# A graph attention layer on one core: four products of zero weights a block between spreading q[dst] and k; the last nodes split into early units and tiles of 128 rows; powers ahead of the copies of rows

## The chip, the cores and the metric

The kernel runs on one core of a Trainium2 chip. The metric is the device time of one execution in microseconds (us); a time is given as the median of several executions. The core has five engines, each with an instruction stream of its own: TensorE (PE; its weight loads are listed as PEld), VectorE (DVE), ScalarE (ACT), GpSimd (POOL) and SyncE (SP), which here issues most of the DMAs. A core has 16 DMA engines.

## The reference

12,500 nodes of 128 features, 212,500 edges sorted by their destination `dst`, 8 heads of 16 features. With h = relu(layernorm(x)):

```python
q, k, v = h @ Wq.T + bq, edge_attr @ Wk.T + bk, h @ Wv.T + bv
in_m   = sum(q[src] * k)        # per edge and head
out_m  = sum(q[dst] * k)
diag_m = sum(q[src] * q[dst])
score = (segsoftmax(in_m / 4) + segsoftmax(out_m / 4) + segsoftmax(diag_m / 4)) * weight ** lam
y = segment_sum(score[..., None] * v[dst], dst) @ Wo.T + bo
out = x + leaky_relu(y, 0.1)
```

`segsoftmax` is a softmax over the edges of one destination. Inputs and outputs are float32.

## The kernel before

**Stages.** `ordered_path` first computes layernorm and q of all nodes and writes q to a table in DRAM (until about 160 us). Then comes the loop over the edges, which takes most of the time, and then the end of the program behind the loop, called the tail here. Beside it stands a general path, which runs only if the data have not the expected order.

**The loop.** The edges lie in 5 segments (S) of 83 tiles (G), and one block is 512 edges of one segment: `for g in range(end)` with 415 blocks, segment s = g % 5, tile t = g // 5. The iteration of block g computes the logits of block g and prepares what later blocks need:

- POOL: `gather(g + 23)`, four indirect DMAs (L696) that fetch q[src] of 128 edges each into a tile `qq`. Each is made to start behind a certain product of PE: `behind[g, 0]` to `behind[g, 3]` are the ends of `spread_q`, `project`, `turn` and of the rest of the iteration.
- PE: `spread_q(g + 1)` (L1201), four bf16 products of one-hot rows `oh` with a window of the q table, which put q[dst] and the bias of k into the two halves of `kq_ps` (a PSUM tile of two banks, two such tiles in turn); then `project(g + 1)` (L1190), float32 products that add edge_attr @ Wk into the k half; then `turn(g + 2)` (L1183), four transposes of edge rows into `eT_ps` (one such tile).
- ACT: the copy `eT` (L1185) of `eT_ps`, which `project` of the next iteration reads; the copy `qd` (L1194) of q[dst], behind `project`; the one-hot rows `relb`, `oh` (L1177, L1178).
- DVE, `logits(g)`: the products `prod` of qd with k (L1215) and of qq with both halves of `kq_ps` (L1216); every second block the sums over 16 features, `lT` (L1220).

Spread over the five blocks of a tile lies the work on whole tiles, for tiles that are one to three behind: `turn_logits` transposes `lT` into `l_ps` (L1241), two scans (L1274, L1292) find the running maximum of each destination from both sides, `turn_max` turns it back (`m_ps`, L1366), `powers` takes the exponentials (`back`, L1376 and L1377), `weigh_powers` multiplies them by the weights (L1387), `show_ends` makes the selection `sel` (products `d_ps`, L1402), `to_rows` sums the exponentials of each destination by 16 products (`w_ps`, L1417) and copies them out (`rows`, L1423), and `put_rows` writes windows of 38 node rows for each segment to the DRAM tables `sums` (L1434).

**The nodes.** Units of 256 nodes are worked off by `Nodes` objects, two units (four tiles of 128 rows) each: `load_sums` reads numerators and denominators (L1088; L1090 where a unit lies on the border of two segments and has two parts), `scores_of` divides (L1057 to L1063), `product` computes v by a bias product and four float32 products (L1113, L1115), `hold` does this into a PSUM place that is kept, `weigh` multiplies v by the scores (L1123), `turn` transposes (L1107), `project_o` multiplies by Wo (the same two product lines), `take_larger` and `add_x` finish (L1138, L1142), `store` writes (L1148, L1150). Of 25 such objects 20 are worked off within the loop, from t = 18 on. The others, `rest`, are [18,9], [10,19], [28,29], [38,39] and [48]: their x is loaded and normalized within the last 12 blocks (`begin_rest`), their sums are loaded behind the last rows.

**What sets the order.** Every instruction is pinned: each engine runs its instructions in the order in which the code writes them, and waits on semaphores where data or a buffer are needed. SP issues its DMAs in the same order. The order of the tail is thus the order of the calls at the end of `ordered_path`, and the places of the loop's products that of the calls within the loop.

Of the kernel before, what the change touches and what calls it, by code (L numbers as in the profile page):

```python
# [16 lines left out]
HEADS = 8  # L17
# [455 lines left out]
def ordered_path(ctx: ExitStack, tc: tile.TileContext, flag, x, src, dst, edge_attr, edge_weight,  # L473
# [48 lines left out]

    def parts_of(u):

        return [s for s in range(S)
                if (s == 0 or START * s - NEAR < UN * (u + 1))
                and (s == S - 1 or UN * u <= START * (s + 1) + NEAR)]

    def stored_at(u):

        of = parts_of(u)
        t = -(-(UN * (u + 1) + NEAR - START * of[0]) // RATE)
        return t + 2 if len(of) == 1 and t < T else None

# [7 lines left out]
    sums = [dram.tile([NP, 2, 2 * H3], F32, name=f"sums{i}") for i in range(S)]  # L542

# [43 lines left out]
    worst = consts.tile([RW, 1], F32, name="worst")  # L587
    LEAD, RAW, AHEAD = 3, 15, 11
# [467 lines left out]
    def scores_of(ab, score):  # L1056
        pin(nc.vector.tensor_add(ab[:, :, 0, :], ab[:, :, 0, :], ab[:, :, 1, :]))  # L1057
        den, num = ab[:, :, 0, 0:H3], ab[:, :, 0, H3:]
        pin(nc.vector.tensor_scalar(den, den, 1e-30, None, op0=ALU.max))
        pin(nc.vector.reciprocal(den, den))  # L1060
        pin(nc.vector.tensor_mul(num, num, den))
        pin(nc.vector.tensor_add(score, num[:, :, 0:HEADS], num[:, :, HEADS:2 * HEADS]))
        pin(nc.vector.tensor_add(score, score, num[:, :, 2 * HEADS:]))  # L1063

    class Nodes:
# [13 lines left out]
        def load_sums(self, to=None, more=None):  # L1079
            self.ab = fin.tile([P, JN, 2, 2 * H3], F32, name="ab", bufs=3) if to is None else to  # L1080
            for i, u in enumerate(self.of):
                both = slice(2 * i, 2 * i + 2)
                of = parts_of(u)

                def rows(s):
                    return (sums[s][u * UN:(u + 1) * UN].rearrange("(p k) i c -> p k (i c)", p=P))

                pin(nc.sync.dma_start(self.ab[:, both].rearrange("p k i c -> p k (i c)"), rows(of[0])))  # L1088
                if len(of) > 1:
                    pin(nc.sync.dma_start(more[:, both].rearrange("p k i c -> p k (i c)"), rows(of[1])))  # L1090
# [49 lines left out]
        def add_x(self, engine):  # L1140
            v, y = self.held[:, :self.n], self.x[:, :self.n]
            pin(engine.tensor_add(y, v, y))  # L1142

        def store(self):
            for i, u in enumerate(self.of):
# [3 lines left out]
                else:  # L1149
                    pin(nc.sync.dma_start(out[u * UN:, :].rearrange("(p k) f -> p (k f)", k=2),  # L1150
                                          y[:LAST, :]))


# [4 lines left out]
    rest = [u for _, u in todo] + [u for u in range(NU) if stored_at(u) is None]  # L1158
    rest = [Nodes(rest[i:i + 2]) for i in range(0, len(rest), 2)]

    with tc.tile_pool(name="work", bufs=2) as work, \
# [43 lines left out]

        def logits(g):
# [7 lines left out]
            prod = prods[0][:, :, s - lo]  # L1214
            pin(nc.vector.tensor_mul(prod[:, :, 2, :], qds[g], kqs[g][:, :, 1, :]))  # L1215
# [3 lines left out]
            if s % 2 == 0 or alone:  # L1219
# [7 lines left out]
        ends_ab = scan.tile([P, len(rest) * JN, 2, 2 * H3], F32, name="ends_ab", bufs=1)  # L1227
# [95 lines left out]
        def examine():  # L1323
# [31 lines left out]
            pin(nc.vector.tensor_reduce(found[:, 3:4], found[:, 0:3], AX.X, ALU.max))  # L1355
            pin(nc.vector.tensor_copy(flag, found[:, 3:4]))
# [13 lines left out]
        def powers(t):  # L1370
            d = st[t]
            back = d["back"] = work.tile([P, JN, S, 2, H3], F32, name="back")
# [79 lines left out]
        def nodes_between(t, s):  # L1452
# [17 lines left out]
            if old and even and s == 2:  # L1470
                old.take_larger()
                old.add_x(nc.vector)
# [6 lines left out]
        assert len(rest) <= len(starts)  # L1479
# [5 lines left out]
        def begin_rest(at):  # L1485
            if at in turned:
                late.update(zip(turned[at], halves(len(turned[at]))))
            for r, (of, begin) in enumerate(zip(rest, starts)):
                if at == begin:
                    to, of.h = halves()  # L1490
                    of.load_x(to)
# [5 lines left out]

            if at == BEGIN - 1:
                for of in rest:
                    of.more = None  # L1500
                    if any(len(parts_of(u)) > 1 for u in of.of):
                        more = gath.tile([P, JN, F], F32, name="qq").rearrange("p j f -> p (j f)")
                        of.more = more[:, :of.n * 4 * H3].rearrange(
                            "p (k i c) -> p k i c", k=of.n, i=2)
                        pin(nc.gpsimd.memset(of.more, 0.0))
# [28 lines left out]
        for g in range(end):  # L1534
# [5 lines left out]
            if g + 1 < end:  # L1540
                spread_q(g + 1)
                behind[g + 1, 0] = pinned[products]
                project(g + 1)
# [28 lines left out]
            elif t < G - 1:  # L1572
                later(to_rows, t - 2)
# [21 lines left out]
            if g == end - 1:  # L1595
                last_pair.turn(small([P, JN, P], "node_ps"))
                more_banks()
            if g < S:
                of = [u for u in range(NU) if g in parts_of(u)]
# [126 lines left out]
```

## Time and profile before

| what | value |
|---|---|
| median of 3 runs | 2637.92 us (2632.82 to 2642.26) |
| the profiled execution's own time | 2642.74 us |
| its span, first to last instruction | 2640.9 us |
| mean granted TensorE clock | 0.786 of full speed |
| last gather of q[src] issued | about 2472 us |
| last put of rows issued | 2603.65 us |
| last addition on DVE ends | 2633.85 us |
| last store issued | 2634.72 us |

Before about 162 us the tables are made; to about 2588 us the loop runs; behind it lies the tail. The profile's page lists each engine's busy time, the granted clock (`PEclk`) in 40 slices of the span, and groups of instructions by line; lists of waits name, for each engine and line, what ended the idle time ahead of it.

### The profile page before, as it was taken

What the parts mean: (1) busy time and instruction counts of PE and PEld (TensorE: products, weight loads), DVE (VectorE), ACT (ScalarE), POOL (GpSimd) and SP (SyncE); (2) the same over time, 40 slices, a digit from 0 to 9 for tenths busy, and PEclk for the clock granted to TensorE, in tenths of its full rate; (3) what the DMA queues carried; (4) which work ended last, traced back from release to release, by engine and by line L of the source; (5) the groups of instructions that cost most, each with busy time, mean ns of one, the idle gap of its engine ahead of it and who ended that gap; (6) DMA issues with size and microseconds to landing.
All of it is one profiled execution on the core that took longest, in us unless ns stands there. A gap on an engine that the chain in (4) does not pass through costs nothing.

```text
span 2640.9 us, 34648 instructions
## 1 busy us (share of the span) xinstructions
PE 1657.0 (63%) x9986; PEld 1406.9 (53%) x9986; DVE 2002.2 (76%) x2205; ACT 1422.5 (54%) x2742; POOL 1587.3 (60%) x1678
## 2 busy tenths in 40 slices
PE   5655656565665566666666666565666666666677
PEld 4544545454555455555555565454555555555665
DVE  6656777777787777777878777777877787778896
ACT  6644555455555555555555555555554555555572
POOL 6666666666666666666666666666666666666200
PEclk9876777778777887877878777878877787778786
DMA  8464444444444444444444444444444444444431
GB/s 235 143 202 130 132 121 121 145 131 121 129 147 132 131 132 148 140 132 130 134 139 144 126 134 144 144 122 130 146 139 129 124 145 139 120 126 133 122 91 53
DMA packets 306303, 355.74 MB, mean 135 GB/s; under 512 B 118433, under 2 KB 225899, under 8 KB 305795
## 3 DMA queue, kind: packets, MB, share of 16 engines
q1 hardware_dynamic: 238340, 238.99, 29.8%
q0 software_dynamic: 53184, 108.92, 15.0%
q10 hardware_dynamic: 14580, 5.53, 0.8%
q8 instruction: 82, 1.34, 0.2%
q14 instruction: 117, 0.96, 0.1%
HBM read 321.41 MB, written 31.85 MB: 134 GB/s over the span
## 4 chain that ended last, share of the span: by engine, by line
PE 31%; ACT 22%; another core or an unknown queue 17%; issue 14%; DVE 10%; DMA 0%; DVEq 0%; POOL 0%; ACTq 0%; SPq 0%; POOLq 0%
PE kq_ps L1190 11%; PE w_ps L1417 6%; PE kq_ps L1201 5%; ACT qd L1194 4%; ACT eT L1185 4%; PE eT_ps L1183 4%; ACT relb L1177 4%; DVE lT L1220 3%; DVE prod L1216 3%; ACT oh L1178 2%; PE node_ps L1115 2%; ACT sel L1406 2%; ACT sel L1405 2%; ACT back L1377 1%
## 5 line engine op out<-in xcount | busy, mean ns | idle before, releaser
L696 POOL DMA_INDIRECT qq<-q_table,src_i x1600 | 1517.2, 948 | 852.1 <-issue 368.8
L1190 PE MATMUL kq_ps<-wk,eT 128*128 128x128 f32 x3320 | 627.3, 348 | 677.0 <-ACT eT L1185 478.3
L1190 PEld LDWEIGHTS kq_ps<-wk,eT 128*128 128x128 f32 x3320 | 554.3, 252 | 757.7 <-ACT eT L1185 526.3
L1220 DVE TENSOR_REDUCE lT<-prod 128x192 f32<-128x3072 f32 (+1 forms) x250 | 702.3, 2809 | 8.5
L1194 ACT COPY qd<-kq_ps 128x512 f32<-128x512 f32 x415 | 242.0, 583 | 723.2 <-remote 443.9
L1216 DVE TENSOR_TENSOR prod<-qq,kq_ps 128x1024 f32<-128x1024 f32 x415 | 504.0, 1214 | 0.0
L1215 DVE TENSOR_TENSOR prod<-qd,kq_ps 128x512 f32<-128x512 f32 x415 | 283.1, 682 | 179.5 <-issue 97.5
L1201 PE MATMUL kq_ps<-win,oh 114*128 114x256 bf16 x1660 | 296.5, 307 | 96.8 <-issue 44.5
L1185 ACT COPY eT<-eT_ps 128x512 f32<-128x512 f32 x415 | 244.5, 589 | 174.8 <-remote 117.0
L1183 PE MATMUL eT_ps<-ident,ea 128*128 128x128 f32 x1660 | 321.4, 329 | 5.6 <-issue 5.6
L1177 ACT ACTIVATE relb<-relb,before 114x512 bf16<-114x512 bf16 x415 | 301.8, 727 | 0.0
L1201 PEld LDWEIGHTS <-oh 114*128 114x128 bf16 x1660 | 178.1, 111 | 172.6 <-issue 136.8
L1178 ACT ACTIVATE oh<-relb 114x512 bf16<-114x512 bf16 x415 | 261.5, 630 | 13.2
L1183 PEld LDWEIGHTS eT_ps<-ident,ea 128*128 128x128 f32 x1660 | 258.8, 175 | 6.2 <-issue 6.2
L1417 PE MATMUL w_ps<-back,sel 128*114 128x144 f32 (+1 forms) x1312 | 208.6, 323 | 72.4 <-ACT sel L1406 52.7
L1387 DVE TENSOR_TENSOR back<-back,m_ps 128x480 f32<-128x480 f32 x84 | 54.9, 653 | 256.1 <-ACT back L1377 239.3
L1417 PEld LDWEIGHTS w_ps<-back,sel 128*114 128x114 f32 x1312 | 194.3, 219 | 99.4 <-ACT sel L1406 72.7
L1274 DVE TENSOR_TENSOR_SCAN u<-far,u,l_ps 120x512 f32<-120x512 bf16 x82 | 104.5, 1275 | 30.0 <-PE kq_ps L1201 12.4
L1292 DVE TENSOR_TENSOR_SCAN m<-far_ps,head,u 120x512 f32<-120x512 f32 x81 | 103.9, 1282 | 8.4
L1423 ACT COPY rows<-w_ps 114x240 f32<-114x240 f32 x84 | 29.8, 355 | 129.1 <-PE kq_ps L1201 43.3
L696 POOL DMA_INDIRECT qq<-in_x_dram,raw_i x60 | 61.5, 1024 | 35.7 <-issue 15.6
L1366 PE MATMUL m_ps<-ident,m 120*128 120x120 f32 x332 | 70.1, 351 | 5.5 <-DVE m L1292 2.8
(196 smaller groups left out, 1458.8 us busy)
## 6 DMA issues: line engine op xcount, KB each, us to landing
ea<-in_edge_attr_dram SPq DMA_DIRECT2D x83, 1280.0 KB
relb<-rel_d SPq DMA_DIRECT2D x83, 640.0 KB
qq<-q_table,src_i POOLq DMA_INDIRECT x1600
win<-q_table SPq DMA_DIRECT2D x415, 28.5 KB
far<-far_d SPq DMA_DIRECT2D x84, 120.2 KB
q_table<-more_q SPq DMA_DIRECT2D x40, 192.0 KB
sums<-rows SPq DMA_DIRECT2D x408, 7.1 KB
q_table<-xq SPq DMA_DIRECT2D x24, 256.0 KB
```

Of the source, the lines that this page charges most:

```text
L696: rows = pin(nc.gpsimd.indirect_dma_start(out=qq[:, j, :], out_offset=None, in_=x if g < RAW else q_table, in_offset=bass.IndirectOffsetOn ...
L1177: pin(nc.scalar.activation(d, d, AF.Abs, bias=before[:K3]))
L1178: pin(nc.scalar.activation(oh, d, AF.Relu, bias=1.0, scale=-1.0))
L1183: pin(nc.tensor.transpose(eT_ps[:, j, :], eas[g // S][:, g % S, j * F:(j + 1) * F], ident))
L1185: pin(nc.scalar.copy(eT, eT_ps))
L1190: pin(nc.tensor.matmul(kqs[g][:, j, 1, :], eTs[g][:, j, :], wk, start=False, stop=(j % 2 == 1)))
L1194: pin(nc.scalar.copy(qds[g], kqs[g][:, :, 0, :]))
L1201: pin(nc.tensor.matmul(kq[:, j].rearrange("p i f -> p (i f)"), ohs[g][:, j * P:(j + 1) * P], win[:, s:S + 1:S - s, :], start=(j % 2 == 0), ...
L1215: pin(nc.vector.tensor_mul(prod[:, :, 2, :], qds[g], kqs[g][:, :, 1, :]))
L1216: pin(nc.vector.tensor_mul(prod[:, :, 0:2, :], qqs[g][:, :, None, :].to_broadcast([P, JN, 2, F]), kqs[g]))
L1220: pin(nc.vector.tensor_reduce(lTs[t][:, :, lo:s + 1, :].rearrange("p j s c -> p j (s c)"), prods[0][:, :, :s + 1 - lo].rearrange("p j s i ...
L1417: pin(nc.tensor.matmul(w_ps[:, own[0]:own[-1] + 1, :].rearrange("p s c -> p (s c)"), d["sel"][:n, j, lo:lo + TRIO, :].rearrange("p s w -> ...
```

## The change

Line numbers of the kernel after the change are given with "after".

**Zero products.** A new function `add_nothing(g + 1, 2)` is called in each iteration between `spread_q` and `project` (after: L1278). It issues four bf16 products of 512 columns, two into each bank of the block's `kq_ps`; their weights are the low halves of the float32 identity matrix, which are zero, so they add zero. The first gather of an iteration is still tied to the end of `spread_q`, the second to that of `project`.

**The last nodes.** The borders between segments are now cut at fixed nodes (`CUTS`: 2474, 4974, 7472, 9972), chosen so that a unit's sums lie in one table from a cut on, but for a few nodes around the cut. These are worked off by a new class `Ends`: four tiles of 128 rows, one at each cut, at addresses that are read from the data (`end_bases`, filled in `examine`), whose sums of both tables are added. Their statistics of layernorm go through DRAM (`stats_d`). 21 objects of two units are now worked off in the loop, one more than before (an additional one at t = 14). `rest` is three objects of units 18, 9, 19, 28, 29 and 38, beside `whole` (unit 48) and `ends`.

**The tail.** The sums of the three objects and the second tables' sums of `ends` (14 loads) are now issued ahead of the last three tiles' puts, behind the last put only 5 loads follow (4 of `ends`, 1 of `whole`). `to_rows(G - 3)` moves into the last block's iteration, the products of two held objects ahead of the last `to_rows`, `powers` of the last two tiles ahead of `to_rows(G - 2)`. The last block's sums over features are made in two pieces, the first ahead of the second logits product.

```diff
@@ the loop
                 spread_q(g + 1)
                 behind[g + 1, 0] = pinned[products]
+                add_nothing(g + 1, 2)
                 project(g + 1)
                 behind[g + 1, 1] = pinned[products]
...
-            elif t < G - 1:
+            else:
                 later(to_rows, t - 2)
@@ new
+        halves_of_one = ident.bitcast(BF)
+        nothing = halves_of_one[:, 0:2 * P:2]
+        something = halves_of_one[:, None, :].to_broadcast([P, JN // 2, 2 * P])
+
+        def add_nothing(g, times):
+
+            for i in range(times):
+                for j in range(0, JN, 2):
+                    pin(nc.tensor.matmul(kqs[g][:, j:j + 2].rearrange("p j i f -> p j (i f)"),
+                                         nothing, something, start=False, stop=False))
@@ class Ends
+        def rows(self, t, s):
+            return t[bass.ds(self.base[s], P)]
+
+        def load_sums(self, to, beyond):
+            for s in range(SP1):
+                pin(nc.sync.dma_start(to[:, s].rearrange("p i c -> p (i c)"),
+                                      self.rows(sums[s + beyond].rearrange("n i c -> n (i c)"), s)))
@@ logits
             pin(nc.vector.tensor_mul(prod[:, :, 2, :], qds[g], kqs[g][:, :, 1, :]))
+            if g == end - 1:
+                add_up(2, 3)
@@ the tail
         leaving.store()
+        for r, of in enumerate(rest):
+            of.load_sums(shares(r)[0])
+        ends.load_sums(ends.beyond, 1)
+        halves_of(last_pair.ab, nc.gpsimd)
+        halves_of(ends_ab[:, :first], nc.gpsimd)
+        halves_of(ends.beyond, nc.gpsimd)
+        put_rows(G - 3)
         turn_logits(G - 1)
+        last_pair.project_v(banks.pop(0))
         scan_on(G - 1)
-        to_rows(G - 3)
-        put_rows(G - 3)
         scan_back(G - 2)
         turn_max(G - 2)
-        last_pair.project_v(banks.pop(0))
+        hold(rest[1])
         scan_on(G)
         powers(G - 2)
         scan_back(G - 1)
         turn_max(G - 1)
-        weigh_powers(G - 2)
         scan_back(G)
         turn_max(G)
+        hold(rest[2])
+        weigh_powers(G - 2)
         powers(G - 1)
         powers(G)
+        to_rows(G - 2)
+        put_rows(G - 2)
         weigh_powers(G - 1)
-        to_rows(G - 2)
+        to_rows(G - 1)
+        put_rows(G - 1)
         weigh_powers(G)
-        put_rows(G - 2)
-        for t in (G - 1, G):
-            to_rows(t)
-            put_rows(t)
-        last_pair.scores()
-        last_pair.weigh(last_pair.held)
-        hold(rest[1])
+        to_rows(G)
+        put_rows(G)
+        ends.load_sums(ends_ab[:, after:], 0)
+        whole.load_sums(ends_ab[:, first:after])
...
-        for r, of in enumerate(rest):
-            of.load_sums(ends_ab[:, r * JN:r * JN + of.n], of.more)
...
+        for of in rest[:2]:
+            of.weigh(of.held)
+            of.turn(small([P, JN, P], "node_ps"))
...
+        hold(whole)
+        hold(ends, True)
...
+        both = (ends, whole)
+        for of in both:
+            of.weigh(of.held)
+            of.turn(small([P, JN, P], "node_ps"))
...
+        for of in both:
+            of.project_o(small([P, JN, F], "node_ps"))
+        for of in both:
+            of.take_larger()
+            of.add_x()
+            of.store()
```

In a block in the middle of the loop PE's rows before are these (`win` is the window of the q table, `wk` the weights of k, `ea` edge rows; a row's operands are output<-inputs, and what it waits for stands in brackets):

```order
L1201 LDWEIGHTS oh
L1201 MATMUL kq_ps<-win_108,oh 128x256
L1201 LDWEIGHTS oh
L1201 MATMUL kq_ps<-win_108,oh 128x256
L1190 MATMUL kq_ps<-wk,eT 128x128 [waits Activation_49]
L1190 MATMUL kq_ps<-wk,eT 128x128 x3
L1183 MATMUL eT_ps<-ident,ea 128x128 [waits DMAHW7_49,PE_49]
L1183 MATMUL eT_ps<-ident,ea 128x128 x3
```

and after the change the same place reads:

```order
L1265 LDWEIGHTS oh
L1265 MATMUL kq_ps<-win_109,oh 128x256
L1278 LDWEIGHTS ident
L1278 MATMUL kq_ps<-ident 128x512
L1278 LDWEIGHTS ident
L1278 MATMUL kq_ps<-ident 128x512
L1278 LDWEIGHTS ident
L1278 MATMUL kq_ps<-ident 128x512
L1278 LDWEIGHTS ident
L1278 MATMUL kq_ps<-ident 128x512
L1254 MATMUL kq_ps<-wk,eT 128x128 [waits Activation_49]
L1254 MATMUL kq_ps<-wk,eT 128x128 x3
```

Four pairs of weight load and product of 512 columns now stand between the last row of `spread_q` and the first k product, which waits for ACT's copy `eT` as before.

At the end of the last block, and from there into the tail, PE's rows before are these (`ends_t` belongs to `show_ends`, `h` to a node transpose):

```order
L1402 LDWEIGHTS ends_t_104
L1402 MATMUL d_ps<-shows,ends_t_104 128x380 [waits DVE_49]
L1107 MATMUL node_ps<-ident,h 128x128 [waits Activation_49]
L1107 MATMUL node_ps<-ident,h 128x128
L1107 MATMUL node_ps<-ident,h 128x128 [waits Activation_49] x2
L1241 MATMUL l_ps<-ident,lT 120x128 [waits DVE_49,Activation_49]
L1241 MATMUL l_ps<-ident,lT 120x128 x3
L1417 MATMUL w_ps<-back,sel 114x144 [waits Activation_49]
L1417 MATMUL w_ps<-back,sel 114x144 x3
L1417 MATMUL w_ps<-back,sel 114x96 x4
L1366 MATMUL m_ps<-ident,m 128x120 [waits DVE_49,Activation_49]
L1366 MATMUL m_ps<-ident,m 128x120 x3
```

and after the change:

```order
L1515 MATMUL w_ps<-back,sel 114x144 [waits DVE_49,PE_49,Activation_49]
L1515 MATMUL w_ps<-back,sel 114x144 x3
L1515 MATMUL w_ps<-back,sel 114x96 x4
L1500 LDWEIGHTS ends_t_105 [waits DMAHW7_49]
L1500 MATMUL d_ps<-shows,ends_t_105 128x380
L1500 LDWEIGHTS ends_t_105
L1500 MATMUL d_ps<-shows,ends_t_105 128x380 [waits PE_49]
L1130 MATMUL node_ps<-ident,h 128x128 [waits Activation_49]
L1130 MATMUL node_ps<-ident,h 128x128 x3
L1326 MATMUL l_ps<-ident,lT 120x128 [waits DVE_49,Activation_49]
L1326 MATMUL l_ps<-ident,lT 120x128 x3
L1136 LDWEIGHTS ones_89
```

The 16 products `w_ps` of tile G - 3 have moved from behind the transposes `l_ps` to a place ahead of the last `d_ps` products and of `l_ps`.

On SP, the end of the last put and the loads behind it before (rows that issue no DMA are left out):

```order
L1434 DMA sums_71<-rows 38x48 [waits DMAHW7_49]
L1088 DMA ends_ab<-sums_68 128x192 [waits DMAHW5_49,DMAHW0_49]
L1088 DMA ends_ab<-sums_67 128x192 [waits DMAHW1_49]
L1090 DMA qq<-sums_68 128x192 [waits DMASW6_49,DMASW1_49,DMASW7_49,DMASW0_49,Pool_49]
L1088 DMA ends_ab<-sums_67 128x192
L1090 DMA qq<-sums_68 128x192 [waits DMASW4_49,DMASW3_49,DMASW5_49,DMASW2_49,Pool_49]
L1088 DMA ends_ab<-sums_68 128x192 [waits DMAHW2_49]
L1090 DMA qq<-sums_69 128x192 [waits DMAHW3_49]
L1088 DMA ends_ab<-sums_69 128x192 [waits DMAHW4_49]
L1090 DMA qq<-sums_70 128x192 [waits DMASW6_49,DMASW7_49,DMASW1_49,DMAHW5_49,DMASW0_49,Pool_49]
L1088 DMA ends_ab<-sums_69 128x192 [waits DMAHW6_49]
```

and after, where the `ISA` rows load the addresses of the cuts:

```order
L1532 DMA sums_71<-rows 38x48 [waits DMAHW5_49]
L1203 ISA
L1203 DMA ends_ab<-sums_67 128x96 [waits DMAHW7_49,DMAHW3_49]
L1203 ISA
L1203 DMA ends_ab<-sums_68 128x96 [waits DMAHW6_49]
L1203 ISA
L1203 DMA ends_ab<-sums_69 128x96 [waits DMAHW1_49]
L1203 ISA
L1203 DMA ends_ab<-sums_70 128x96 [waits DMAHW0_49]
L1111 DMA ends_ab<-sums_71 128x192 [waits DMAHW2_49]
```

Of 16 loads, 5 are left behind the last put, and the `qq` loads of second parts are gone from there.

More of the change, by code (lines that the diff above doesn't have):

```diff
@@ L587, in ordered_path @@
     worst = consts.tile([RW, 1], F32, name="worst")
+    end_bases = consts.tile([1, SP1], I32, name="end_bases")
     LEAD, RAW, AHEAD = 3, 15, 11
@@ L1637, in ordered_path @@
         last_pair.take_larger()
-        last_pair.add_x(nc.vector)
+        last_pair.add_x()
         last_pair.store()
-        more_banks()
-        for r in (2, 3):
-            hold(rest[r])
-        banks.append(last_pair.v)
-        hold(rest[4])
-        score = scan.tile([P, len(rest) * JN, HEADS], F32, name="end_score", bufs=1)
-        tiles = [r * JN for r in range(len(rest))] + [sum(of.n for of in rest)]
-        def add_more(r, engine):
-            if rest[r].more is not None:
-                some = ends_ab[:, tiles[r]:tiles[r + 1]]
-                pin(engine.tensor_add(some, some, rest[r].more))
@@ new lines, in ordered_path @@
+        rest[0].add_x()
+        rest[0].store()
+        rest[1].project_o(small([P, JN, F], "node_ps"))
+        halves_of(ends_ab[:, first:], nc.vector)
+        pin(nc.vector.tensor_add(ends_ab[:, after:, 0, :], ends_ab[:, after:, 0, :],
+                                 ends.beyond[:, :, 0, :]))
+        inverse_of(ends_ab[:, first:])
+        heads_of(ends_ab[:, first:], score[:, first:], nc.vector)
+        whole.score, ends.score = score[:, first:after], score[:, after:]
+        both = (ends, whole)
```

208 lines of the change are left out of this document (139 added, 69 removed).

## The prediction

> **What bounds the kernel now.** I read the page's totals first, then the mean clock and busy time of two long stretches, then the waits, then single stretches of the loop, and last the chain of waits at the end.
>
> ```profile
> span 2640.9 us, 34648 instructions
> PE 1657.0 (63%) x9986; PEld 1406.9 (53%) x9986; DVE 2002.2 (76%) x2205; ACT 1422.5 (54%) x2742; POOL 1587.3 (60%) x1678
> PEclk9876777778777887877878777878877787778786
> PE 31%; ACT 22%; another core or an unknown queue 17%; issue 14%; DVE 10%; DMA 0%; DVEq 0%; POOL 0%; ACTq 0%; SPq 0%; POOLq 0%
> ```
>
> No engine is full, DVE comes nearest with 76%, and the chain that ended last changes hands between PE, ACT and an unnamed releaser. So the loop is paced by a ring of waits. TensorE runs at 7 to 8 tenths of its clock nearly throughout.
>
> The next rows split the time at the last gather (columns: stretch, its length, busy time and count of PE, PEld, DVE, ACT, POOL, then clock, DMA share, GB/s); in the second pair of rows only L1215 is counted, which runs once a block.
>
> ```profile
> 162.00:2471.00 2309.00, 1434.76 (x8720) 1222.26 (x8721) 1764.17 (x1661) 1227.38 (x2311) 1479.70 (x1563) 0.78 0.46 135
> 2471.00:2579.40 108.40, 78.19 (x517) 67.74 (x516) 100.26 (x92) 80.14 (x157) 3.22 (x6) 0.86 0.32 98
> ...
> 162.00:2471.00 2309.00, 266.81 (x391) 0.78 0.46 135
> 2471.00:2579.40 108.40, 14.98 (x22) 0.86 0.32 98
> ```
>
> While gathers run, a block takes 2309 / 391 = 5.905 us at clock 0.78; without them 108.4 / 22 = 4.93 us at 0.86, with DVE 92% busy. Gathers, or something that goes with them, cost 0.98 us a block. Their own engine isn't full either:
>
> ```profile
> L696 POOL DMA_INDIRECT qq<-q_table,src_i x1600 | 1517.2, 948 | 852.1 <-issue 368.8
> ...
> PEld kq_ps L1190 <- ACT eT L1185: 526.3, 157, 8.7
> ...
> ACT qd L1194 <- remote: 443.9, 101, 12.3
> ...
> POOL qq L696 <- remote: 222.7, 149, 2.7
> PEld kq_ps L1190 <- issue: 209.8, 75, 8.2
> ...
> DVE prod L1215 <- issue: 97.5, 52, 3.9
> ...
> DVE prod L1215 <- ACT qd L1194: 68.0, 43, 10.7
> ```
>
> (Columns of the waits: total us, times, longest us.) Four gathers of 0.95 us are 3.8 us of a block of 5.9; each is held behind a PE product. In 157 + 75 = 232 of 415 blocks the first k product (L1190) waits, by 735.8 / 232 = 3.2 us on average. ACT's copy L1194 then waits for that product, by a releaser which the trace can't name, 443.9 us in 101 blocks. PE stands still just ahead of the point where the new products go.
>
> **The zero products: do they lift the clock?** One such stall shows the clock. Columns of the first two rows are as above.
>
> ```profile
> 1229.00:1230.00 1.00, 0.00 (x0) 0.00 (x0) 0.86 (x3) 0.00 (x0) 0.82 (x1) 1.00 1.03 401
> 1232.00:1233.00 1.00, 0.00 (x0) 0.00 (x0) 0.00 (x0) 0.42 (x1) 0.69 (x2) 0.50 1.05 373
> ...
> 1228.28 0.60 PE L1201 MATMUL kq_ps<-win,oh 114*128 114x256 bf16 x4
> 1236.05 1.22 PE L1190 MATMUL kq_ps<-wk,eT 128*128 128x128 f32 x4 [7.17 <-ACT eT L1185]
> ```
>
> PE stops at 1228.88 and is idle for 7.17 us; in the fourth microsecond of it the clock has dropped to half. So a mean wait of 3.2 us is near what it takes, and 0.9 us of work ahead of each wait would save some of the drops, not all: waits reach 8.7 us. [...]
>
> What is a higher clock worth? Of 14 stretches of 25 blocks each (310 to 2375 us; L1215 alone is counted), these are the three of the highest clock, the three at 0.80 and the two of the lowest.
>
> ```profile
> 310.50:457.50 147.00, 17.07 (x25) 0.76 0.44 130
> ...
> 603.90:755.70 151.80, 17.10 (x25) 0.80 0.44 129
> 755.70:896.90 141.20, 17.00 (x25) 0.81 0.46 138
> 896.90:1045.50 148.60, 17.08 (x25) 0.80 0.46 136
> ...
> 1342.50:1488.00 145.50, 17.05 (x25) 0.80 0.47 139
> 1488.00:1641.50 153.50, 17.08 (x25) 0.76 0.45 134
> 1641.50:1785.60 144.10, 17.03 (x25) 0.83 0.47 136
> ...
> 2083.50:2228.60 145.10, 17.00 (x25) 0.84 0.45 133
> ```
>
> Means: 143.5 us at 0.81 to 0.84, 148.6 at 0.80, 150.3 at 0.76. The loop's own mean is 25 x 5.905 = 147.6. If the clock made the whole difference, lifting all 391 blocks (15.6 stretches) to the upper group would give 15.6 x (147.6 - 143.5) = **-64 us**. But the link is loose: 145.5 occurs at 0.80, 147.0 at 0.76, and fewer stalls make a high clock as well as a high clock makes fewer stalls. Below, the bound is nothing gained. I take near half, **-30 us**.
>
> **What the zero products cost.** Each block gets 4 products of 512 columns. The trace has none; the nearest are bf16 products of 380 columns, alone and in pairs.
>
> ```profile
> 1215.59 0.81 PE L1402 MATMUL d_ps<-shows,ends_t 21*128 21x380 bf16 x2
> ...
> 1242.64 0.49 PE L1402 MATMUL d_ps<-shows,ends_t 21*128 21x380 bf16 x2
> ...
> 2482.28 0.32 PE L1402 MATMUL d_ps<-shows,ends_t 21*128 21x380 bf16 x1 [1.59 <-DVE x_in L1142]
> ```
>
> At full clock a second one adds 0.49 - 0.32 = 0.17 us, so 512 columns 0.17 x 512 / 380 = 0.23, and four 0.92 us. At half clock: 0.81 - 0.49 = 0.32, 0.43 for 512, 1.72 for four. PE has room: 415 x 0.92 = 382 us on 1657 busy. In the 232 blocks with a wait ahead of L1190 the products lie in that wait and cost nothing. In the other 183 they push L1190, the transposes behind it and the gather held behind it by 0.92 us. Whether that reaches the end depends on who is late next. Bounds: 0 where the ring has slack behind it (DVE is idle 24% of the time; POOL spends 3.8 us on gathers and 368.8 / 400 = 0.9 us on their issue of 5.9 a block, which leaves 1.2), and 183 x 0.92 = +168 us where it has none. I take 0, because a product pushed at full clock is bounded by the slack of DVE in most blocks: L1215 waits for this path in only 52 + 43 = 95 of 415.
>
> **The tail and the node work.** These pieces are of the chain that ended last, but for the DVE row, which is of DVE's timeline (start, length, what).
>
> ```profile
> 2586.66 1.76 DVE lT L1220
> ...
> 2589.64 3.43 PE w_ps L1417 x16
> ...
> 2603.65 1.23 DMA sums<-rows
> ...
> 2605.32 0.42 SPq L1088
> ...
> 2607.75 3.19 DMA qq<-sums
> ...
> 2609.73 0.70 DVE L1138 TENSOR_TENSOR node_ps<-h,node_ps 128x512 f32<-128x512 f32 x1 [6.42 <-ACT h L1134]
> ...
> 2622.11 0.87 PE node_ps L1107 x4
> ...
> 2623.63 0.58 PE node_ps L1113
> 2624.22 2.01 PE node_ps L1115 x8
> ...
> 2633.43 0.42 DVE qq L1142
> ```
>
> Before, 16 loads go out behind the last put of rows; the first sums are added at 2611.1, 7.4 us after the put (2603.65), and DVE stands idle for 6.42 us ahead of 2609.73. Six groups of nodes, the last pair among them, have a transpose of four tiles (0.87 us) and a product (0.58 + 2.01) there: 3.5 us of PE each. After, ten loads of sums go out earlier, so that the work of three groups fits into that idle stretch, and only 5 loads are behind the last put. Then PE's own sum is what binds: from 2603.7 the last pair and three groups, 4 x 3.5, two products held for the last nodes, 2.6 and half of it, the four cut tiles, 3.5, and the last unit, half of that: 14 + 3.9 + 5.3 = 23.2. With about 1 us of the last additions it ends at 2627.9, where before it ended at 2633.43 + 0.42 = 2633.9: **-6 us**. The 16 w_ps products (3.43 us) leave their place behind l_ps and go ahead of it, beside the reduction that ended at 2588.42: between -3.4 (they leave the chain) and +3.4 (l_ps waits for them); I take **-3**, since their powers are those of a tile two tiles back. Two held products (2.6 each) move ahead of the last w_ps products; one can lie beside the scans, and with the other I take **+4**, of 0 to 5.2. On SP, 14 loads go ahead of the third-last put and delay it by up to 14 x 0.42 = 5.9 us; no step of the chain above starts from that put, so I count nothing. Together **-5 us**. Bounds: with the loads alone as the limit (five issues of 0.42 from 2604.9, 3.2 to land, then some 10.5 us for one group's additions, transpose, product and ends) it ends at 2621, -13; with nothing gained and all of 3.4 and 5.2 lost, +9.
>
> The one further pair of units in the loop and the small additions (copies of the statistics, the addresses of the ends, twelve loads of the ends) cost next to nothing: 25 blocks ahead of the first pair of units took 147.0 (310.50 to 457.50), the loop's mean is 147.6, and 2.5 pairs fall on 25 blocks, so one costs 0.6 / 2.5 = 0.2 us; the small additions run once, on queues with idle time. I take 0, at most a microsecond or two.
>
> **Sum** against the profiled execution (2642.74 us, of which 2640.9 is its span; 4.8 us over the median of the three runs): 2642.7 - 30 - 5 = **2608**.
>
> **Rivals.**
> (1) The loop is paced by the gathers' holds and by ACT's and DVE's waits, not by PE's clock: it keeps its 5.905 us, only the tail moves. For: the unnamed releaser leads the waits, and 0.80 stands at both 145.5 and 151.8. Against: the upper group is 5 us below. Time 2642.7 - 5 = 2638.
> (2) The clock stays nearly full: all of -64, time 2574. For: the mean wait is only just as long as the drop takes. Against: waits up to 8.7 us.
> (3) Slower: the zero products lie on the path. In the 95 blocks where DVE waited for the copy behind L1190, each is later by 0.92 us: +87, time 2642.7 + 87 - 5 = 2725. It decides if these blocks are mostly such in which PE didn't wait for eT; at half clock (1.72) it would be more. For: nothing sits between these products and the copy but L1190; the gather behind L1190 is late too. Against: PE waits there in 232 blocks, and the added work is small beside the 3.2 us.
>
> **How the numbers follow.** Partial gain 0.38, (1) 0.25, (2) 0.17, (3) 0.20. Range: down to 2550, which is (2) with the tail's other bound (2574 - 8 = 2566) and a quarter of the 64 below it, since the 4.93 us a block without gathers show that the upper group is no floor; up to 2680, which is (1) with half of the 87 paid (2638 + 43). That leaves out the upper half of (3), and little else. Within 0.3% (8 us, about what a measurement of this kernel can tell from no change) is most of (1): with a small share of (1) on either side and of the others, faster 0.58, same 0.20, slower 0.22.
>
> **What would show it.** Right: the mean clock of the loop at 0.83 or more, L1190's wait down by about 0.9 us where it stood, and 25 blocks at 145 to 146 us. Case (1): clock up, blocks as before. Case (3): fewer and shorter waits of L1190 but more waits of the copy L1194 and of L1215. The tail: from the last rows' put to the last add under 25 us (before: 2603.7 to 2633.9, 30.2). I am wrong if the clock falls, or if the gathers' waits change by more than the products' length.

## The result, and the profile after

| | before | after |
|---|---|---|
| median | 2637.79 us (2632.82 to 2645.04, 6 runs) | 2657.53 us (2652.95 to 2665.24, 6 runs) |
| profiled execution | 2642.74 us | 2665.24 us |
| mean granted clock | 0.786 | 0.837 |

The ratio after to before is 1.0073, 95% interval [1.0052, 1.0094]: the change costs about 20 us. The forecast was 2608 us.

The page of the kernel after begins thus (span, busy time of each engine, the clock in 40 slices, the chain that ended last by engine):

```profile
span 2663.5 us, 38138 instructions
PE 1952.3 (73%) x11668; PEld 1522.4 (57%) x11668; DVE 2004.8 (75%) x2219; ACT 1425.0 (54%) x2749; POOL 1586.8 (60%) x1675
PEclk9777888888888888888888879888887888878998
PE 39%; ACT 19%; another core or an unknown queue 17%; issue 12%; DVE 11%; DMA 0%; DVEq 0%; ACTq 0%; POOL 0%; SPq 0%; POOLq 0%
```

PE is busy 295 us longer, and the clock stands mostly at 8 where it stood mostly at 7. DVE, ACT and POOL are busy as long as before. The stretch of the first 391 blocks, between the same products of DVE as before (stretch, length, busy time and count of PE, PEld, DVE, ACT, POOL, then clock, DMA share, GB/s):

```profile
165.00:2494.40 2329.40, 1722.49 (x10308) 1336.42 (x10309) 1768.37 (x1677) 1228.66 (x2316) 1479.87 (x1563) 0.84 0.46 134
```

It takes 2329.4 us where it took 2309.0, so 20.4 of the 22.6 us of span are the loop's; 25 blocks take 148.9 us, not 147.6. The waits (total us, times, longest):

```profile
ACT qd L1258 <- remote: 561.3, 123, 9.8
PEld kq_ps L1254 <- ACT eT L1249: 388.8, 126, 7.0
...
POOL qq L709 <- remote: 238.7, 154, 2.3
...
PEld kq_ps L1254 <- issue: 164.3, 97, 5.9
...
DVE prod L1296 <- issue: 116.6, 53, 3.9
...
DVE prod L1296 <- ACT qd L1258: 82.6, 55, 9.3
```

The first k product waits 553 us in 223 blocks, 2.5 us each, where it waited 736 in 232, 3.2 each. That part went as meant. But ACT's copy `qd` behind it waits 117 us longer for its unnamed releaser (`remote`), and DVE 15 us longer for that copy and 19 us longer for nothing that the profile names (`issue`).

In the tail, the last tile's puts of rows begin at 2631.7 and DVE's last addition ends at 2655.8 (ACT's queue, then DVE; start, length, what):

```profile
2631.74 0.69 ACTq L1532 DMA_DIRECT2D sums<-rows  x2
...
2655.34 0.42 DVE L1165 TENSOR_TENSOR qq<-node_ps,qq 128x256 f32<-128x256 f32 x1
```

That is 24.0 us, against 30.2 before (2603.65 to 2633.85). But from the last block's first logits product (2584.82 before, 2610.83 after) to these puts it is 20.9 us, against 18.8. The chain of waits after the change shows where:

```profile
2611.01 0.85 ACT sel L1504
2611.90 3.51 PE w_ps L1515 x16
...
2615.86 0.66 PE node_ps L1130 x4
...
2616.99 1.29 DVE u L1359
```

The last reduction and the first scan, in the timeline of DVE, before and after (in brackets the idle time ahead):

```profile
2586.66 1.75 DVE L1220 TENSOR_REDUCE lT<-prod 128x96 f32<-128x1536 f32 x1
2589.68 1.28 DVE L1274 TENSOR_TENSOR_SCAN u<-far,u,l_ps 120x512 f32<-120x512 bf16 x1 [1.26 <-PE l_ps L1241]
```

```profile
2613.39 1.22 DVE L1291 TENSOR_REDUCE lT<-prod 128x64 f32<-128x1024 f32 x1
2616.99 1.28 DVE L1359 TENSOR_TENSOR_SCAN u<-far,u,l_ps 120x512 f32<-120x512 bf16 x1 [2.38 <-PE l_ps L1326]
```

The 16 products that moved ahead of `l_ps` are still in the chain. They start when ACT has finished `sel` (2611.9) and end at 2615.4, 0.8 us behind the last reduction (2614.6). Behind them come the `d_ps` products, the transposes `node_ps` and only then `l_ps`, so the scan begins 2.4 us after the reduction, where it began 1.3 us after it before.

### The profile page after: what moved, and what is told of

Read it like the earlier page. It is cut to its first block, busy times and chain, and to the rows that moved or that the text cites. A ratio compares the mean times of both kernels' runs of the same rounds, so it can differ in the third digit from the quotient of the medians.

```text
span 2663.5 us, 38138 instructions
## 1 busy us (share of the span) xinstructions
PE 1952.3 (73%) x11668; PEld 1522.4 (57%) x11668; DVE 2004.8 (75%) x2219; ACT 1425.0 (54%) x2749; POOL 1586.8 (60%) x1675
## 4 chain that ended last, share of the span: by engine, by line
PE 39%; ACT 19%; another core or an unknown queue 17%; issue 12%; DVE 11%; DMA 0%; DVEq 0%; ACTq 0%; POOL 0%; SPq 0%; POOLq 0%
PE kq_ps L1254 10%; PE w_ps L1515 6%; PE kq_ps L1265 6%; PE kq_ps L1278 6%; DVE lT L1305 4%; ACT qd L1258 4%; PE eT_ps L1247 4%; ACT eT L1249 4%; ACT relb L1241 3%; DVE prod L1299 3%; PE node_ps L1138 2%; ACT sel L1503 1%; ACT sel L1504 1%; ACT oh L1242 1%
## 5 line engine op out<-in xcount | busy, mean ns | idle before, releaser
L1254 PE MATMUL kq_ps<-wk,eT 128*128 128x128 f32 x3320 | 563.8, 324 | 463.0 <-ACT eT L1249 326.5
L1254 PEld LDWEIGHTS kq_ps<-wk,eT 128*128 128x128 f32 x3320 | 517.9, 230 | 596.3 <-ACT eT L1249 388.8
L1278 PE MATMUL kq_ps<-ident 128*128 128x512 bf16 x1656 | 467.5, 406 | 9.9 <-issue 9.5
L1265 PE MATMUL kq_ps<-win,oh 114*128 114x256 bf16 x1660 | 286.6, 299 | 54.8 <-DVE prod L1299 21.9
L1247 PE MATMUL eT_ps<-ident,ea 128*128 128x128 f32 x1660 | 308.7, 318 | 10.1 <-DVE qq L971 6.3
L1278 PEld LDWEIGHTS <-ident 128*128 128x128 bf16 x1656 | 173.2, 105 | 148.4 <-issue 48.6
L1247 PEld LDWEIGHTS eT_ps<-ident,ea 128*128 128x128 f32 x1660 | 245.6, 168 | 10.0 <-DVE qq L971 6.5
L1265 PEld LDWEIGHTS <-oh 114*128 114x128 bf16 x1660 | 172.7, 108 | 123.5 <-issue 87.8
```

Source lines behind the costliest of these rows:

```text
L1247: pin(nc.tensor.transpose(eT_ps[:, j, :], eas[g // S][:, g % S, j * F:(j + 1) * F], ident))
L1254: pin(nc.tensor.matmul(kqs[g][:, j, 1, :], eTs[g][:, j, :], wk, start=False, stop=(j % 2 == 1)))
L1265: pin(nc.tensor.matmul(kq[:, j].rearrange("p i f -> p (i f)"), ohs[g][:, j * P:(j + 1) * P], win[:, s:S + 1:S - s, :], start=(j % 2 == 0), ...
L1278: pin(nc.tensor.matmul(kqs[g][:, j:j + 2].rearrange("p j i f -> p j (i f)"), nothing, something, start=False, stop=False))
```

## The experiments

Each kernel was timed beside the kernel before on the same chip; ratios are to that. Differences in us are the ratio's share of the time before; those of the medians are up to 3 us away from them. Three sets of runs fell on chips where the kernel before takes 2637 to 2638 us, as in the result, and two on chips where it takes 2160 to 2161. This was not foreseen, and much of the explanation rests on it.

**What part of the change costs: a_nozero, b_zero4, b_zero8, b_zero4_first.** The first is the kernel after without its products, the others are the kernel before with products alone.

```diff
# a_nozero, from after
-                add_nothing(g + 1, 2)
# b_zero4 from before (b_zero8: add_nothing(g + 1, 4))
                 behind[g + 1, 0] = pinned[products]
+                add_nothing(g + 1, 2)
                 project(g + 1)
# b_zero4_first from before, in spread_q
             kq = banks_of(g)
+            if g > 0:
+                for i in range(2):
+                    for j in range(0, JN, 2):
+                        pin(nc.tensor.matmul(kq[:, j:j + 2].rearrange("p j i f -> p j (i f)"),
+                                             nothing, something, start=True, stop=True))
```

> The kernel after the change without its zero products; all else as after. Theory Z (the zero products cost what the change lost, the rest is worth about -5 us): about 2633 us, ratio to before 0.998, with the mean clock back at 0.78 to 0.79. Rival O (the zero products are neutral, the other edits cost the time): about 2657 us, ratio 1.007.

> The kernel before with nothing but the four zero products a block, at the place of the change. Theory Z: about 2661 us (before plus 23), ratio 1.009, clock 0.83 to 0.84, and the loss lies in the loop (blocks 0 to 391 longer by about 20 us). Rival O: 2638 us, ratio 1.000.

> The kernel before with eight zero products a block at the same place. Z with no gain from the clock (each product costs only the part of its length that lies on the path): the loss doubles, about +45 us, 2683 us. Z with a real gain from the clock that four products had nearly used up (cost of four about 50 to 80, gain 30 to 60): the second four cost 50 to 80 without a gain, 2710 to 2740 us. Clock 0.90 or more in both. Rival O: 2638 us.

> The kernel before with the four zero products ahead of the products of q[dst] (spread) instead of behind them, so that the first gather of each block, too, is held 0.9 us longer; the clock gets the same work. If the cost is the delay of the k product, it is the same here, about 2661 us. If the gathers' holds carry it, it is more, 2680 us or above. If four products cost only where they stand (between spread and k), it is less, 2640 to 2650 us.

| kernel | us | ratio, 95% interval | clock |
|---|---|---|---|
| before | 2636.63 | | |
| a_nozero | 2636.18 | 0.9997 [0.9985, 1.0010] | 0.786 |
| b_zero4 | 2657.99 | 1.0081 [1.0064, 1.0099] | 0.837 |
| b_zero8 | 2678.90 | 1.0168 [1.0149, 1.0187] | 0.937 |
| b_zero4_first | 2649.53 | 1.0051 [1.0033, 1.0069] | 0.853 |

The zero products are the whole loss, and all the other edits together are worth nothing that can be measured (theory Z; O falls). Eight products bring the clock to 0.94 and cost twice as much as four (44 and 21 us):

```profile
PEclk9788899999999999999999999999998999998997
...
L1214 PE MATMUL kq_ps<-ident 128*128 128x512 bf16 x3312 | 827.9, 387 | 67.1 <-issue 65.5
```

(Group of the zero products of b_zero8: busy us, mean ns of one, idle ahead.) The gathers' holds don't carry the cost, since holding one gather more costs less (b_zero4_first, 1.0051 against 1.0081), not more.

**Where a product stands, and what is paid: b_s03x8, b_s12x8, b_short4, b_short16.**

```diff
# b_s03x8, from b_zero4; b_s12x8: in (1, 2)
+                if (g + 1) % S in (0, 3):
+                    add_nothing(g + 1, 4)
# b_short4, from b_zero4; b_short16: add_nothing(g + 1, 8)
-                    pin(nc.tensor.matmul(kqs[g][:, j:j + 2].rearrange("p j i f -> p j (i f)"),
-                                         nothing, something, start=False, stop=False))
+                    pin(nc.tensor.matmul(kqs[g][:, j, 1, 0:16],
+                                         nothing, halves_of_one[:, 0:16], start=False, stop=False))
```

> The kernel before with eight zero products at the same place, but only in the blocks of segments 0 and 3, where the first k product waited 2.7 and 2.95 us on average in the kernel before (1328 products in all, 0.8 of those of the change). Theory S (the clock is worth little; PE time added to the ring is paid at a small share, where PE doesn't wait): clock about 0.83, 2637 to 2645 us. Rival H (the clock gives back some 60 us, and four products a block cost some 85 on the path): the gain without most of the cost, 2600 to 2620 us. Rival I (the cost goes with the number of PE instructions): plus 17, 2654 us.

> As the run before, but in the blocks of segments 1 and 2, where the first k product waited 0.3 and 1.0 us: the same number of products and nearly the same heat. S: more than with segments 0 and 3, plus 25 to 40, about 2670 us. H: far more, plus 60 to 100. I: the same as with segments 0 and 3, 2654 us.

> The kernel before with four zero products a block of 16 columns instead of 512: as many instructions and weight loads as the change, about a third of its time, hardly any work for the clock. S: plus 3 to 7, about 2642 us, clock 0.79. I: plus 21, 2658 us. H: a third of the 85 without a gain, plus 28, 2665 us.

> The kernel before with sixteen zero products a block of 16 columns: about the time of the four products of the change, with little of their work, so that the delay comes without the warm clock. S: plus 15 to 25, about 2658 us, with the clock not above 0.80. H: the whole cost without the gain, plus 80 or more, 2720 us. I: plus 84, 2720 us.

These runs fell on a chip where the kernel before takes 2161.03 us, so that the expectations in us don't apply, only their order.

| kernel | us | ratio, 95% interval | clock |
|---|---|---|---|
| b_s03x8 | 2159.29 | 0.9989 [0.9981, 0.9998] | 0.908 |
| b_s12x8 | 2230.72 | 1.0325 [1.0310, 1.0340] | 0.848 |
| b_short4 | 2162.45 | 1.0000 [0.9992, 1.0009] | 0.850 |
| b_short16 | 2160.32 | 0.9995 [0.9983, 1.0006] | 0.881 |

The windows of 391 blocks of b_short4, which is as quick as the kernel before, show what is different there (columns as above; of the kernel before there is no trace on such a chip):

```profile
119.00:1987.70 1868.70, 1380.29 (x10287) 1208.25 (x10288) 1752.97 (x1661) 1215.46 (x2310) 1412.97 (x1493) 0.85 0.56 166
```

The same work of DVE (1753 us, before 1764) fills 94% of 1869 us, not 76% of 2309. The list of waits of b_short16, for one, holds no row with an unnamed releaser for the copy `qd`, which had 443.9 us of it in the kernel before. I read this as DVE bounding the loop there. Sixteen short products a block cost nothing that can be measured (0.9995). Eight long ones in the blocks of segments 1 and 2 cost 70 us; in those of 0 and 3 they cost nothing, and with a clock of 0.908 the time is 0.1% less (interval 0.02% to 0.2%). The place counts (1.0325 against 0.9989), the higher clock hardly (0.908, where the runs of the kernel before have 0.81 to 0.83). In b_s12x8 DVE's first product waits for the copy behind k, 99.3 us in 83 blocks, which it does for 13.8 us in b_short16:

```profile
DVE prod L1226 <- ACT qd L1194: 99.3, 83, 4.2
```

```profile
DVE prod L1226 <- ACT qd L1194: 13.8, 7, 3.6
```

On this chip the k product's own wait isn't what makes the place: ahead of it PE stands still for 0.06 us or less on average in the blocks of every segment of b_short4 (12.1 us in 11 blocks is all that its list of waits has for ACT's copy). PE's room is. Between the starts of `spread_q` of segments 1 and 2, PE or its weight loads are busy 5.03 of 5.04 us in b_s12x8, and 2.78 of 2.98 in b_short4 (means of blocks 60 to 360). So nothing is left there to take the products up, and DVE's time from the first logits product of segment 0 to that of segment 1 grows from 3.84 to 4.81 us.

**The same on a chip like that of the result: after_again, s03x8_again, s12x8_again, short16_again.**

> The changed kernel itself. On a chip on which the kernel before takes about 2637 us (PE's completions arrive microseconds late while gathers run): 2657 us again, ratio 1.007. On one on which it takes about 2161 us (completions arrive at once, DVE busy 92%): theory S (a product costs where nobody waits ahead of k, and nothing where PE would have waited) gives a loss between that of segments 0 and 3 (-2 us) and of segments 1 and 2 (+70 us for 1328 products), some +20 to +45 us, ratio 1.010 to 1.020. A rival: DVE is the bound there and hides four products, 1.000, or the tail's edits show as a gain, 0.998.

> Eight zero products only in the blocks of segments 0 and 3, again. On a chip with 2637 us before: S 2637 to 2645 us; H (hidden gain of the clock) 2600 to 2620; I (count of instructions) 2654. On one with 2161 us: 2159 again.

> The same in the blocks of segments 1 and 2. On a chip with 2637 us before: S plus 25 to 40, 2662 to 2677 us; H plus 60 to 100; I 2654. On one with 2161 us: 2231 again.

> Sixteen zero products of 16 columns a block, again. On a chip with 2637 us before: S plus 10 to 25; H and I plus 80. On one with 2161 us: 2160 again.

| kernel | us | ratio, 95% interval | clock |
|---|---|---|---|
| before | 2637.57 | | |
| after_again | 2658.62 | 1.0068 [1.0045, 1.0092] | 0.840 |
| s03x8_again | 2647.07 | 1.0035 [1.0023, 1.0046] | 0.854 |
| s12x8_again | 2666.65 | 1.0114 [1.0088, 1.0139] | 0.833 |
| short16_again | 2701.64 | 1.0237 [1.0214, 1.0260] | 0.779 |

Two parts of the cost show. The place: about as many products (1320 and 1328) cost 9 us in the blocks in which k waits long and 30 in those in which it waits little. H (products on the path cost far more, the clock gives it back) falls with segments 0 and 3, which were to be faster than before. And the number of instructions: sixteen short products have little over half of the four long ones' busy time (263.2 and 459.5 us) and cost three times as much (62.5 and 21.4 us), which S (10 to 25 us) doesn't allow. Their groups on the one chip and on the other (busy us, mean ns | idle ahead, most of it by "issue", that is, waiting for nothing which the profile shows):

```profile
L1214 PE MATMUL kq_ps<-ident 128*128 128x16 bf16 x6624 | 263.2, 171 | 106.4 <-issue 105.3
```

```profile
L1214 PE MATMUL kq_ps<-ident 128*128 128x16 bf16 x6624 | 231.8, 170 | 0.0
```

PE's timeline on the first shows that idle time:

```profile
176.49 0.20 PE L1214 MATMUL kq_ps<-ident 128*128 128x16 bf16 x2 [1.12 <-issue]
177.20 0.17 PE L1214 MATMUL kq_ps<-ident 128*128 128x16 bf16 x1 [0.51 <-issue]
177.91 0.23 PE L1214 MATMUL kq_ps<-ident 128*128 128x16 bf16 x3 [0.54 <-issue]
178.63 0.17 PE L1214 MATMUL kq_ps<-ident 128*128 128x16 bf16 x1 [0.49 <-issue]
```

Sixteen products without a semaphore between them, and PE stands still for 0.49 to 0.54 us after each one, two or three, until the last nine run through. On the other chip no idle time stands ahead of them (0.0 us).

**Time against number of instructions: f32x1, with after_third.** One float32 product replaces four bf16 ones (`zeros` is a tile of zeros).

```diff
# f32x1, from b_zero4; called with add_nothing(g + 1, 1)
+                pin(nc.tensor.matmul(kqs[g][:, 2 * i:2 * i + 2].rearrange("p j i f -> p j (i f)"),
+                                     zeros, ident[:, None, :].to_broadcast([P, JN, P]),
+                                     start=False, stop=False))
```

> The kernel before with one float32 product of zero weights and 512 columns a block at the same place: about the time of the four products of the change, but one instruction of the program a block instead of eight. On a chip with 2637 us before: theory S (time on the path) plus 15 to 25; theory I (each instruction of PE is paid, some 9 us for 1000 pairs of weight load and product, as sixteen short products suggest) plus 2 to 8, 2641 us. On one with 2161 us: S as the change there; I 2161.

> The changed kernel once more, to see it on a chip on which the kernel before takes about 2161 us: S plus 20 to 45 us; if DVE's 92% hides four products, 2161. On a chip with 2637 us before: 2657 again.

On a chip with 2637.99 us before, f32x1 took 2649.35 us, 1.0043 [1.0024, 1.0061], and after_third 2660.46 us, 1.0087 [1.0067, 1.0107]. The time on PE is the same, and the clock nearly (0.850, against 0.838 in after_third); records are 828 against 1656:

```profile
L1216 PE MATMUL kq_ps<-ident,zeros 128*128 128x512 f32 x828 | 460.9, 639 | 2.3 <-issue 2.3
```

```profile
L1214 PE MATMUL kq_ps<-ident 128*128 128x512 bf16 x1656 | 459.5, 401 | 3.9 <-issue 3.9
```

(the second is of b_zero4). About half of the loss goes, at the same time on PE, with fewer instructions: the 11 us lie between S (15 to 25) and I (2 to 8), and neither holds alone. Two constants describe the runs on such chips. From b_zero4 (1.656 thousand pairs of weight load and product, 459.5 us busy, +21.4 us) and short16_again (6.624 thousand, 263.2 us, +62.5) come 8.9 us per thousand pairs and 0.015 us per us of product. They give 41 for b_zero8 (measured 44), 14 for f32x1 by its 828 records (11), and 17 for the mean of s03x8_again and s12x8_again (20), but 22 for b_zero4_first (13). By this estimate some 15 of the 21 us are paid for the number of instructions and 7 for time, and the place moves that by 10 either way. It is no more than an estimate: the idle time ahead of the products, which should show the number, is 106 us in short16_again and 67 in b_zero8, but 4 in b_zero4.

**The change on a chip of the other kind: after_fourth.**

> The changed kernel, for a chip on which the kernel before takes about 2161 us. There sixteen short products cost nothing and eight long ones in the blocks of segments 1 and 2 cost 70 us: if a product is paid by its time where PE is not waited out, plus 20 to 45 us, ratio 1.010 to 1.020; if DVE's 92% hides four products a block, 1.000. On a chip with 2637 us before: 1.007 to 1.009 again.

It fell on a chip with 2160.15 us before: 2163.23 us, 1.0014 [0.9996, 1.0032]. The loop's 391 blocks take what b_short4's take, with PE 131 us busier and the clock at 0.93 for 0.85:

```profile
118.90:1987.30 1868.40, 1511.48 (x10305) 1209.37 (x10306) 1756.58 (x1677) 1219.48 (x2317) 1409.21 (x1492) 0.93 0.57 166
```

Its waits are led by ACT's for the k product and PE's for nothing named and for DVE; the unnamed releaser is not in the list.

```profile
ACT qd L1258 <- PE kq_ps L1254: 418.4, 309, 5.9
PEld L1265 <- issue: 347.4, 231, 4.0
PE kq_ps L1265 <- DVE prod L1299: 284.3, 204, 3.8
```

So the change gains nothing there either, and costs nothing that can be measured: as I read it, DVE, at 94% of the loop, covers it; no run varied DVE's work.

## Why the prediction was wrong

- **What bounds the loop.** It was read as a ring of waits in which an unnamed releaser leads. That was right as far as it went. The unnamed releaser of the copy `qd` and of the gathers is PE's own semaphore in every such wait (101 and 149 of them in the kernel before), updated too late for the profile to name the product. From the modelled end of the nearest product that signals to the update of the semaphore, it is 0.84 us in the median in the kernel before and over 3.8 in a tenth (200 to 1900 us of the span), against 0.014 us in b_short4; the updates of DVE and ACT come about 0.01 us behind their ends in both. So in the one trace PE's completions reach ACT and POOL late and in the other they don't, and on the chip of the other the kernel before takes 2161.03 us for 2637.79, 18% less. I took it for the kernel's own and asked what a higher clock would do within it.
- **The step that failed: "What is a higher clock worth?", the term of -30 us.** It came from 14 stretches, in which a high clock went with a short time. The clock did rise as forecast (0.83 or more; 0.84), and the blocks became longer. The link is no price of the clock. a_nozero has nearly the loop of the kernel before, without the products. Its own 14 stretches of the same blocks take 147.5 us on average, and the four of the highest clock 148.2:

```profile
1339.70:1489.40 149.70, 17.02 (x25) 0.81 0.46 136
1489.40:1639.00 149.60, 17.00 (x25) 0.81 0.46 137
...
1783.90:1932.30 148.40, 17.07 (x25) 0.82 0.45 134
1932.30:2077.40 145.10, 17.05 (x25) 0.83 0.47 140
```

  The correlation of time and clock over the stretches is -0.5 in the kernel before, 0.0 in a_nozero, and between -0.6 and 0.2 in all kernels on such chips. What does come again is which blocks are short: the three stretches that the prediction took for the high clock (143.5 us) are below the mean in each of these kernels, at whatever clock (a_nozero 145.6 us at 0.77, mean 147.5; b_zero8 147.3 at 0.96, mean 149.4). So in part the upper group was short by its blocks, and in part by chance. On the chips where the kernel before takes 2160 us, the granted clock went from about 0.82 (runs of the kernel before) to 0.93 and the time did not change (after_fourth, 1.0014); on those of the result b_zero8's 0.937 came with +44 us. Rival (1) had this right.
- **The zero products' cost, taken as 0, is +21 us.** Their length was right: 0.86 us a block in the chain of the kernel after (L1278), 0.92 forecast. The first k product's wait fell by 0.7 us, 0.9 forecast. The term was put at 0 because DVE's slack was to cover a push; on these chips it didn't, and the cost had a part that the prediction left out: the number of instructions (f32x1, short16_again). The bounds, 0 to +168, held it; rival (3), +87, gave the sign and four times the size. What takes up the rest of a delay no run shows.
- **The tail, forecast -5 us, is not measurable** (a_nozero 0.9997). The step behind the last put has the right size, 24.0 us for 30.2, -6.2 against -6, but in part by luck: PE's own work was to fill 23.2 us there and to bind. From 2631.7 to 2654.9 PE is busy 18.1 us of 23.2, and one wait of it, for DVE's work on the sums that are loaded last, is 2.3 us:

```profile
2646.16 1.54 PE L1130 MATMUL node_ps<-ident,qq 128*128 128x128 f32 x6 [2.29 <-DVE qq L1146]
```

  The step ahead of it was wrong: the 16 `w_ps` products were to save 3 us by leaving their place behind `l_ps`, but in that place they lay beside the two scans. In the kernel before the second scan, which the transposes `m_ps` need, ends at 2592.60, and these begin at 2592.86:

```profile
2591.32 1.28 DVE L1292 TENSOR_TENSOR_SCAN m<-far,head,u 120x512 f32<-120x512 bf16 x1
2592.86 1.01 PE L1366 MATMUL m_ps<-ident,m 120*128 120x120 f32 x4
```

  By these rows the old place cost half a microsecond at most, and in the new one the products delay `l_ps`. With the two held products, the time to the last put grew by 2.1 us, against +1 in the sum. What is left is less than the tails differ among themselves: from the last block's first logits product to the end, the kernels with the old tail took 51.2 to 56.0 us on such chips, those with the new one 51.8 to 53.0.
- **The extra pair and the small additions at 0**: a_nozero doesn't speak against it; it shows them only together with the tail.
- The profiled execution's first block comes 2.9 us later than before (165.0 for 162.1); in the other kernels on such chips it begins between 157.8 and 162.6, so this is no part of the change.

What stays open: why completions come late on some chips, whether that and the half-microsecond gaps of short16_again have one cause, and how much of the 18% they make. On those chips the clock's worth isn't separated from the products' time in the runs with more products: the 0.015 us per us is what is left of both.

## What to carry to other kernels

Filler products that raised TensorE's mean clock bought nothing here that could be measured, at 0.84 (b_zero4, 1.0081) and 0.94 (b_zero8, 1.0168) on the one kind of chip and at 0.93 (after_fourth, 1.0014) on the other, and the filler's instructions and place cost from nothing (b_short16, 0.9995) to 3% (b_s12x8, 1.0325). What a higher clock is worth where TensorE's own speed bounds the time was not shown. A correlation between clock and time within one trace is no price: look first whether a second execution shows it again. And where the profile's leading waits have no named releaser, measure on another chip before tuning against them.

## What the runs showed of the hardware

- The same program takes 2657 to 2660 us on some chips and 2163 on another (after, after_third; after_fourth), with nearly equal busy time of DVE in 391 blocks (1768 us in after, 1757 in after_fourth). One gather takes 948 ns on average on the first kind (after) and on the second (b_short16).
- On the first kind, the updates of PE's semaphore come 0.84 us in the median behind the modelled ends of products (before), on the second 0.014 us (b_short4).
- On the first kind 6624 pairs of weight load and short product came with +62.5 us, about 9 us per thousand (short16_again), on the second with nothing that can be measured (b_short16, 0.9995).
- A float32 product of 512 columns took as long as four bf16 ones of 512 (460.9 us in f32x1, 459.5 in b_zero4, in all) in half as many records (828 and 1656).
- On the second kind the mean clock was 0.881 with sixteen products of 16 columns in every block (b_short16), 0.850 with four of them (b_short4), 0.908 with eight of 512 columns in the blocks of segments 0 and 3 (b_s03x8) and 0.848 with as many in those of segments 1 and 2 (b_s12x8).
